# A table of steps for the pieces around a scan, and fp8 products in place of fp32 transposes

## The chip, the core and the metric

The kernel runs as one program on one NeuronCore of a Trainium2 chip. The core has a matrix engine (PE; its weight loads are shown apart as PEld), a vector engine (DVE), an activation engine (ACT), a general engine (POOL) and a queue that only issues transfers (SP). Each works through its own list of instructions in the order in which the program wrote them. The metric is device time in microseconds (us), start to end of one execution; the median of three runs is given for the kernel before.

## What is computed

The input x is 4 images of 64 x 64 tokens with 96 channels, fp32. Two layers follow.

Layer 0 is a group norm over the whole image (32 groups of 3 channels), a layer norm, a projection of 96 to 4896 columns, and a scan over the 4096 tokens with 16 states per channel:

```python
h_new = d * (A_t * h) + d * (B_t * u)          # 96 channels x 16 states
y     = g_t * jnp.sum(C_t * h_new, axis=-1)    # g = sigmoid(gate)
x     = x + (y @ W_out + b_out)
```

Layer 1 is attention without a softmax (so K and V can be contracted first, into one matrix per image), then a feed-forward network whose inputs, weights and hidden values are rounded to fp8 (5 exponent bits, 2 mantissa bits) and whose sums are rounded to fp16:

```python
t = t + attn(ln(t));   t = t + ffn(ln(t))      # ffn: q8(ln) @ q8(W1), relu, q8, @ q8(W2)
```

## The kernel before, in words

**Chunks, tiles and steps.** A batch image is cut into 8 chunks of 512 tokens, so there are 32 chunks. The 96 x 16 = 1536 states of a chunk are cut into 12 tiles of 128 partitions (3 groups of 32 channels times 4 groups of states). One *step* works on one tile, so a chunk is 12 steps and the main loop has K = 384 steps. Step numbers below are relative to the first step of the chunk that a piece belongs to; what counts for who meets whom is the number modulo 12, here called the *residue*.

**What a step holds.** For tile s the program writes, in this order: the B product of tile s+3 (PE, `b_proj`) and its copy out of PSUM (ACT, `b_copy`), the A product of tile s+1 (`a_proj`), the C product of tile s (`c_proj`), a copy of the last state (ACT, `keep`), the product B*u of tile s+2 (POOL, `b_mul`, L751), the scan of tile s (DVE, L767), A*d of tile s+1 (DVE, `a_mul`, L760), C*h of tile s (DVE, `c_mul`, L791), and then the pieces that were registered for this step. Each of the three products is three matmuls of 128 x 512 (high and low parts of fp32 numbers). For 4 of the 12 tiles, `ON_POOL`, C*h is done by ACT (`c_copy`, L797) and POOL (`c_mul_pool`, L800) instead of DVE, one step later. The A product has two PSUM banks: A of tile s+1 can start when the scan of tile s-1 has ended. B has one bank, which `b_copy` frees. All pieces share three banks named M, which go round.

**The pieces.** They are registered with `at(step, function)`, and run in the order of registration within a step.
- `front`: `load_x`, the group norm's `centre` and `scale` (POOL), layer norm (`stats` on DVE, `rstd` on POOL, `apply` on ACT), `transpose` (PE), `affine` and `upper` (ACT), `low` (DVE, then three transfers on SP), the products for d, u and gate with their outputs (`d_out` ACT, `du_out` DVE, `gate_out` ACT), and `write` and `read` (SP), which spread d and d*u over partitions through DRAM. They all run ahead of the chunk's first step.
- `gather` (a POOL transfer that adds) folds the four groups of states into one.
- `tail`: `state_sum` (PE), `gated` (DVE), the output product, `residual`, the norm of layer 1 with its `apply`, `transpose`, `keep` and `spill` (SP, to DRAM), and the Gram matrix of the chunk.
- `attn_matrix`, once per image, turns the Gram matrix into one 97 x 96 matrix.
- `ffn`, one image (96 steps) later: `fetch` (SP), `attention` (PE), `residual`, norm, `apply` (L371, ACT; L378, DVE, in the last image), `transpose` (L996, PE, fp32), `quant_in` (L1000, ACT, PSUM to fp8), three times `hidden` and `relu`, `project_out` (L1035), `round_out`, `bias_out` and `total` (POOL, L1049 and L1055) and `store`.
- `group_norm` for the next image: 8 times `sums`, then a chain of small pieces.

**Buffers.** x of a chunk lies in one of 15 buffers from `load_x` until `total` of its feed-forward part. The queue order on SP is the order in which the steps write its transfers.

**Start and end.** The first six steps are laid out by a small planner (`planned_start`) with costs and due times, and what is left after step 384 by another (`end`): it orders the remaining pieces by rank and by when they can start. `Plan.LOOK` is how far apart two start times still count as equal.

The order of instructions, and so everything below, is set by the program text alone; there is no scheduler behind it.

Of the kernel before, what the change touches and what calls it, by code (L numbers as in the profile page):

```python
# [21 lines left out]
J = 4  # L22
# [15 lines left out]
FRONT = -22  # L38
SUMS = -28
FFN0 = 28  # L40
ON_POOL = (1, 3, 6, 10)
# [4 lines left out]
def conv_attn_hybrid_kernel(  # L46
# [35 lines left out]
        "xn2": 1, "xq": 1, "h16": 1, "hr": 1, "hq": 1, "y16": 1, "yb": 1, "o": 1,  # L82
# [106 lines left out]
    xa_t, xal_t = [], []  # L189
    for r in range(2):  # L190
        t = const.tile([P, J, CA], F32, tag=f"xa{r}", name=f"xa{r}")
        nc.gpsimd.memset(t[:, :, C:CA], 1.0)
        xa_t.append(t)
        t = const.tile([CA, J, P], F32, tag=f"xal{r}", name=f"xal{r}")
        nc.gpsimd.memset(t[C:CA], 1.0)
        xal_t.append(t)

# [12 lines left out]
    w2_sb = sb("xn2", [C, HID], F32, "w2_sb")  # L210
# [125 lines left out]
    class LayerNorm:  # L336
# [32 lines left out]
        def apply(self, dst, src):  # L369
            for j in range(J):  # L370
                nc.scalar.activation(  # L371
                    dst[:, j, 0:C], src[:, j, :], AF.Identity,
                    bias=self.nmr[:, j : j + 1], scale=self.r[:, j : j + 1],
                )

        def apply_vector(self, dst, src):
            for j in range(J):
                nc.vector.tensor_scalar(  # L378
                    dst[:, j, 0:C], src[:, j, :], self.mv[:, j, 0:1], self.r[:, j : j + 1],
                    ALU.subtract, ALU.mult,  # L380
                )
# [182 lines left out]
    def group_norm(b, s0):  # L564
        q = {}

        def make():
            q["g"] = GroupNorm(b)
            q["g"].first()

        def call(name, *args):
            getattr(q["g"], name)(*args)

        when = [s0 + SUMS + NT * n for n in range(NCH)]
        if b == 1:
            when = [8, 15, 22, 29, 36, 43, 50, 57]
        if b > 1:
            at(when[0] - 7, load_gx, b, 0)  # L580
        at(when[0] - 2, make)
        for n in range(NCH):
            if n:
                at(max(when[n] - 7, when[n - 1]), load_gx, b, n)
            at(when[n], call, "sums", n)
        for n, name in ((1, "moments"), (2, "mean"), (4, "root"), (6, "diagonal"), (8, "spread"),
                        (8, "spread_out")):
            at(when[-1] + n, call, name)
# [107 lines left out]
    def front(b, i, s0, f=None):  # L696
        s = s0 + FRONT
        if f is None:
            f = Front(b, i)
            if (b, i) not in xt:  # L700
                at(s - 3, load_x, b, i)
            at(s, f.centre, nc.gpsimd)
            at(s + 1, f.scale, nc.gpsimd)
            at(s + 2, f.stats)
            at(s + 3, f.ln.rstd)
            at(s + 5, f.apply)
            at(s + 7, f.transpose)
            at(s + 8, f.affine)
            at(s + 9, f.upper)
            at(s + 9, f.low)  # L710
            at(s + 12, f.proj, 2)
            at(s + 13, f.d_out)
            at(s + 13, f.proj, 0)
            at(s + 14, f.du_out)
            at(s + 14, f.write)
            at(s + 15, f.read)
        at(s + 20, f.proj, 1)
        at(s + 21, f.gate_out)
# [89 lines left out]
    def state_sum(g, last=None, first=None):  # L808
# [17 lines left out]
        {"A": 2, "B": 1, "C": 1, "M": 3, "xal": 2, "xat": 1, "bu": 5, "h": 3, "rep": 2,  # L826
# [5 lines left out]
    def tail(b, i, s0):  # L832


        nm, g = f"{b}_{i}", b * NCH + i
        v, ln = {}, LayerNorm(1e-5, f"a_{nm}")
# [46 lines left out]
        def gram_add():  # L883
            nc.gpsimd.tensor_tensor(grams[b], grams[b], v["add"], ALU.add)

        plan = [
            (5, state_sum, g), (6, gated), (7, project_out), (8, residual), (8, ln.stats, t),
            (9, ln.rstd), (12, ln.apply, xa, t), (14, transpose), (15, keep), (16, spill),
            (21, gram), (22, gram_out),
        ]  # L890
        if i:
            plan.append((23, gram_add))
        for n, fn, *args in plan:
            if s0 + n < K:
                at(s0 + n, fn, *args)
        if s0 + plan[-1][0] < K:
            return
# [3 lines left out]
        job, a = end.job, None  # L901
        if s0 == K:
            for sh, late in ((0, 0.0), (2, 0.0), (3, 2.4)):
                w = job(f"wait{sh}", late, lambda: None)
                a = job("PE", 0.5, state_sum, g, sh, sh > 0, after=[a, w],
                        take=["B:y"] if sh == 0 else [])
            a = job("DVE", 0.7, gated, after=[a], free=["B:y"])
            a = job("PE", 0.5, project_out, after=[a], take=["B:o"])
            a = job("DVE", 0.56, residual, after=[a], free=["B:o"])
            a = job("DVE", 1.1, ln.stats, t, after=[a], take=[f"mv:a{i}"])  # L910
            a = job("POOL", 1.3, ln.rstd, False, after=[a])
        else:
            job("wait", 0.0, lambda: None, take=[f"mv:a{i}"])
        if s0 == K:
            applied = job("DVE", 1.3, ln.apply_vector, xa, t, after=[a], free=[f"mv:a{i}"])
        else:
            applied = job("ACT", 1.55, ln.apply, xa, t, free=[f"mv:a{i}"])
        a = job("PE", 0.4, gram, after=[applied, end.last.get("gram")], take=[f"B:g{i}"])
        end.last["gram"] = job("DVE", 0.25, gram_sum, after=[a], free=[f"B:g{i}"])
        a = job("PE", 0.45, transpose, after=[applied], take=[f"C:a{i}"])  # L920
        a = job("ACT", 0.57, keep, after=[a], free=[f"C:a{i}"], take=[f"xat:{i}"])
        end.last[b, i] = job("SP", 0.5, spill, after=[a], late=2.5, free=[f"xat:{i}"])
# [4 lines left out]
    def attn_matrix(b, s0):  # L927
# [31 lines left out]
        for n, (args, out) in enumerate(chain):  # L959
            if s0 < K:  # L960
                at(s0 + 24 + n, mm, *args)
                at(s0 + 24 + n, out)
# [4 lines left out]
    def ffn(b, i, s0):  # L967
# [21 lines left out]
        def apply():  # L989
            v["xn"] = tile_of("xn2", "bu", [P, J, C], F32, "xn2")  # L990
            (ln.apply_vector if b == B - 1 else ln.apply)(v["xn"], t)

        def transpose():
            ps = v["ps"] = bank("C" if phase["end"] else "M", [C, TC], f"xq_ps_{nm}")
            for j in range(J):
                nc.tensor.transpose(ps[:, j * P : (j + 1) * P], v["xn"][:, j, :], ident)  # L996

        def quant_in():
            v["xq"] = tile_of("xq", "h", [C, TC], F8, "xq")
            nc.scalar.activation(v["xq"], v["ps"], AF.Copy, saturate=False)  # L1000
# [7 lines left out]
        def relu(m):  # L1008
            if m == 0:
# [47 lines left out]
        def store():  # L1057
            nc.sync.dma_start(out_v[b, i], v["o"])

        plan = [  # L1060
            (min(-4, K - 4 - s0) if b < B - 1 else 0, fetch),
            (0, attention), (1, residual), (1, ln.stats, t), (2, ln.rstd),
            (5, apply), (7, transpose), (8, quant_in),
            (9, hidden, 0), (10, relu, 0), (11, hidden, 1), (12, relu, 1),
            (13, hidden, 2), (14, relu, 2), (15, project_out), (16, round_out),
            (17, bias_out), (18, total), (19, store),
        ]
        done = [fn for n, fn, *args in plan if s0 + n < K]
        for n, fn, *args in plan:
            if s0 + n < K:  # L1070
                at(s0 + n, fn, *args)
# [5 lines left out]
        assert relu not in done  # L1077
        if fetch in done and attention not in done:
            end.hold(f"xal:{nm}")

        def job(engine, cost, fn, *args, **kw):
            if fn not in done:
                return end.job(engine, cost, fn, *args, **kw)
            return None
# [8 lines left out]
        a = job("DVE" if vector else "ACT", 1.3 if vector else 1.55, apply, after=[a], take=[f"bu:x{nm}"], free=[f"mv:{nm}"])  # L1093
        a = job("PE", 0.45, transpose, after=[a], take=[f"C:{nm}"], free=[f"bu:x{nm}"])
        a = job("ACT", 0.6, quant_in, after=[a], take=[f"h:{nm}"], free=[f"C:{nm}"] if a else [])
        r, h, c = [], None, None
        for m in range(NK):
            h = job("PE", 0.24, hidden, m, after=[a, h], take=[f"M:{m}{nm}"], free=[f"h:{nm}"] if m == 2 else [])
            c = job("ACT", 0.57, round_hidden, m, after=[h, c], take=[f"rep:{nm}"] if m == 0 else [],
                    free=[f"M:{m}{nm}"])  # L1100
            r.append(job("DVE", 0.3, relu_vector, m, after=[c]))
        a = job("ACT", 1.5, quant, after=r, take=[f"bu:q{nm}"], free=[f"rep:{nm}"])
        a = job("PE", 0.5, project_out, after=[a], take=[f"A:y{nm}"], free=[f"bu:q{nm}"])
        a = job(*(("DVE", 0.56) if i % 2 else ("ACT", 0.48)), round_out, after=[a], take=[f"xs:{nm}"], free=[f"A:y{nm}"])
# [10 lines left out]
    def planned_start():  # L1115
        plan = Plan({"A": 2, "B": 1, "C": 1, "D": 1, "M": 3, "bu": 5, "h": 3})
        plan.LOOK = 0.8
# [32 lines left out]
        calm = land("calm", 29.0)  # L1150
# [77 lines left out]
        a = mm(0.5, second.transpose, after=[a, land("then", 38.0)], key="M:x2")  # L1228
# [36 lines left out]
    for b in range(B):  # L1265
        for i in range(NCH):
# [4 lines left out]
            for n, sh in ((7, 1), (10, 2), (13, 3)):  # L1271
                if g < N - 1 or sh == 1:
                    at(s0 + n, gather, g, sh)
            at(s0 + NT, tail, b, i, s0 + NT)
            s = s0 + NCH * NT + FFN0
            at(s - 4 if b == B - 1 else min(s, K) - 4, ffn, b, i, s)
        if b + 1 < B:
            group_norm(b + 1, b * NCH * NT)
        at((b + 1) * NCH * NT, attn_matrix, b, (b + 1) * NCH * NT)
# [82 lines left out]
```

## Time and profile before

| what | value |
|---|---|
| runs | 1212.67, 1214.04, 1214.79 us; median 1214.04 us |
| profiled execution | 1214.51 us, of which the span of instructions is 1212.8 us |
| mean granted PE clock | 0.989 |
| DVE busy | 1125.7 us (93%) |
| PE busy (ends modelled) | 1155.5 us (95%) |
| POOL busy | 1031.6 us (85%) |
| ACT busy | 809.9 us (67%) |
| first scan starts, last scan starts | 30.7 us, 1134.3 us |

A row of the timeline reads: start in us, duration in us, engine, source line, operation, output and inputs by the program's names, shapes, number of instructions merged into the row, and in brackets the idle time before it with what ended it. On DVE the durations overlap by some 0.08 us, so the distance from start to start is what an instruction costs. A row of the windows reads: the stretch and its length, then for PE, PEld, DVE, ACT and POOL busy us with the number of instructions, then the granted clock, the transfers' busy share and GB/s.

### The profile page before, as it was taken

The numbers are of one execution on the slowest core, as the hardware profiler recorded it, in microseconds if no ns is written. First come the engines' busy times: TensorE is split into PE (matmuls) and PEld (weight loads), VectorE is DVE, ScalarE is ACT, GpSimd is POOL, SyncE is SP. The second block draws the span as 40 slices with busy tenths as digits, with TensorE's granted clock in tenths as the row PEclk, the third lists the DMA queues.
The fourth block names the chain that finished last, engine by engine and source line by source line (L and its number), as shares of the span: only waits on it lengthen the run. The fifth ranks groups of instructions, "written<-read, shape, count | busy, mean of one in ns | idle before, by whom it ended". The sixth has DMA issues, their size and how long they took to land. (4 is left out here: it accounts for less than half of the span.)

```text
span 1212.8 us, 19189 instructions
## 1 busy us (share of the span) xinstructions
PE 1155.5 (95%) x5888; PEld 872.8 (72%) x5888; DVE 1125.7 (93%) x2103; ACT 809.9 (67%) x1812; POOL 1031.6 (85%) x1171
## 2 busy tenths in 40 slices
PE   6899999999999999999999999999999999999884
PEld 5677777777777777777777777677777777777652
DVE  6799999999999999999999999999999999999794
ACT  4655656655565787777777777777777777776574
POOL 3988878888888888999999888999999899988654
PEclk8999999999999999999999999999999999999998
DMA  7656767677776676677667766766776667666221
GB/s 185 141 133 145 165 151 164 147 161 164 168 160 151 153 166 151 154 168 176 159 151 164 172 154 146 174 154 149 154 174 154 154 158 174 153 145 142 66 66 40
DMA packets 104289, 182.14 MB, mean 150 GB/s; under 512 B 42637, under 2 KB 50769, under 8 KB 104186
## 3 DMA queue, kind: packets, MB, share of 16 engines
q1 hardware_dynamic: 90060, 106.96, 36.5%
q0 software_dynamic: 13536, 73.93, 30.2%
q8 instruction: 47, 0.77, 0.3%
q14 instruction: 56, 0.46, 0.1%
q10 hardware_dynamic: 590, 0.02, 0.0%
HBM read 69.12 MB, written 24.77 MB: 77 GB/s over the span
## 5 line engine op out<-in xcount | busy, mean ns | idle before, releaser
L751 POOL TENSOR_TENSOR bu<-bu,rep 128x512 f32<-128x512 f32 x384 | 557.7, 1496 | 14.7 <-ACT bu L748 9.2
L748 ACT ACTIVATE bu<-Bps,b_bac 128x512 f32<-128x512 f32 x384 | 263.7, 687 | 286.0 <-PE Bps L244 269.0
L767 DVE TENSOR_TENSOR_SCAN h<-Aps,state,bu 128x512 f32<-128x512 f32 x336 | 426.4, 1269 | 13.2 <-POOL bu L751 3.5
L760 DVE SCALAR_TENSOR_TENSOR Aps<-Aps,b_bac,rep 128x512 f32<-128x512 f32 x384 | 282.5, 736 | 25.1 <-PE Aps L244 24.6
L244 PE MATMUL Bps<-xs,w 128*128 128x512 f32 x768 | 268.1, 430 | 3.7 <-ACT bu L748 3.4
L244 PE MATMUL Aps<-xs,w 128*128 128x512 f32 x768 | 249.6, 406 | 14.2 <-DVE h L767 13.3
L800 POOL TENSOR_TENSOR ch<-ch,h 128x512 f32<-128x512 f32 x128 | 193.5, 1512 | 2.6 <-ACT ch L797 2.4
L244 PEld LDWEIGHTS Aps<-xs,w 128*128 128x128 f32 x768 | 138.6, 189 | 70.5 <-DVE h L767 42.3
L244 PEld LDWEIGHTS Bps<-xs,w 128*128 128x128 f32 x768 | 129.4, 191 | 46.5 <-issue 24.3
L244 PE MATMUL Aps<-xl,w 128*128 128x512 f32 x384 | 152.6, 397 | 0.3 <-DMA w<-w 0.3
L244 PE MATMUL Bps<-xl,w 128*128 128x512 f32 x384 | 151.8, 395 | 0.0
L244 PE MATMUL Dps<-xs,w 128*128 128x512 f32 x384 | 121.1, 397 | 0.0
L244 PE MATMUL Cps<-xs,w 128*128 128x512 f32 x384 | 120.8, 395 | 0.0
L806 POOL DMA_DIRECT2D ch<-ch x94 | 89.0, 947 | 15.1 <-DMA ch<-ch 11.5
L791 DVE SCALAR_TENSOR_TENSOR ch<-Dps,b_bac,h 128x512 f32<-128x512 f32 x128 | 94.7, 740 | 0.5 <-PE Dps L244 0.4
L791 DVE SCALAR_TENSOR_TENSOR ch<-Cps,b_bac,h 128x512 f32<-128x512 f32 x128 | 95.0, 742 | 0.0
L244 PEld LDWEIGHTS Aps<-xl,w 128*128 128x128 f32 x384 | 72.4, 188 | 18.4 <-DMA w<-w 1.0
L244 PEld LDWEIGHTS Bps<-xl,w 128*128 128x128 f32 x384 | 72.5, 189 | 17.5
L244 PEld LDWEIGHTS Dps<-xs,w 128*128 128x128 f32 x384 | 72.4, 189 | 17.5
L244 PEld LDWEIGHTS Cps<-xs,w 128*128 128x128 f32 x384 | 72.3, 188 | 17.5
L244 PE MATMUL Dps<-xl,w 128*128 128x512 f32 x192 | 76.0, 396 | 0.0
L244 PE MATMUL Cps<-xl,w 128*128 128x512 f32 x192 | 75.7, 394 | 0.0
(196 smaller groups left out, 2056.0 us busy)
## 6 DMA issues: line engine op xcount, KB each, us to landing
ch<-ch POOLq DMA_DIRECT2D x94, 768.0 KB, 6.5
rep<-ddd SPq DMA_DIRECT2D x124, 384.0 KB, 6.4
ddd<-dd SPq DMA_DIRECT2D x31, 384.0 KB, 3.0
xl<-lo SPq DMA_DIRECT2D x62, 128.0 KB, 2.4
x<-in_x_dram SPq DMA_DIRECT2D x32, 192.0 KB, 2.9
xatd<-xat SPq DMA_DIRECT2D x32, 192.0 KB, 3.1
xal<-xatd SPq DMA_DIRECT2D x32, 192.0 KB, 5.8
out_dram<-o SPq DMA_DIRECT2D x32, 192.0 KB, 2.1
```

The source lines that it names most:

```text
L244: nc.tensor.matmul(ps, lhsT=wt[:, n], rhs=mv, start=(n == 0), stop=(n == 2))
L748: nc.scalar.activation(self.bu, self.b_ps, AF.Identity, bias=self.bias(0))
L751: nc.gpsimd.tensor_tensor(self.bu, self.bu, rep[self.b, self.i][:, 1, self.cg], ALU.mult)
L760: nc.vector.scalar_tensor_tensor(self.a_ps, self.a_ps, self.bias(1), rep[self.b, self.i][:, 0, self.cg], ALU.add, ALU.mult,)
L767: nc.vector.tensor_tensor_scan(self.h, self.a_ps, self.bu, 0.0 if self.i == 0 else state[self.sh, self.cg], ALU.mult, ALU.add,)
L791: nc.vector.scalar_tensor_tensor(self.slot(), self.c_ps, self.bias(2), self.h, ALU.add, ALU.mult)
L800: nc.gpsimd.tensor_tensor(self.ch, self.ch, self.h, ALU.mult)
L806: nc.gpsimd.dma_start(chs[g, 0], chs.pop((g, sh)), accum_op=ALU.add)
```

## The change

One dictionary `AT` takes the place of the step numbers that were spread over `front`, `tail`, `ffn` and `group_norm`. In steps relative to the chunk's first step, before and after:

| piece | before | after | piece | before | after |
|---|---|---|---|---|---|
| load_x | -25 | -39 | rstd_a | 21 | 21 |
| centre, scale | -22, -21 | -25, -24 | apply_a | 24 | 22 |
| stats, rstd | -20, -19 | -22, -22 | transpose_a, keep, spill | 26, 27, 28 | 33, 34, 39 |
| apply | -17 | -21 | gram, gram_out, gram_add | 33, 34, 35 | 24, 24, 26 |
| transpose, affine | -15, -14 | -14, -13 | fetch | 24 | 21 |
| upper, low | -13, -13 | -13, -12 | attention, residual_f | 28, 29 | 26, 26 |
| proj_d, d_out | -10, -9 | -9, -9 | stats_f, rstd_f | 29, 30 | 26, 27 |
| proj_u, du_out | -9, -8 | -9, -9 | apply_f | 33 | 29 |
| write, read | -8, -7 | -9, -6 | transpose_f, quant_in | 35, 36 | 30, 31 |
| proj_gate, gate_out | -2, -1 | -3, -1 | hidden 0, 1, 2 | 37, 39, 41 | 37, 31, 38 |
| gather 1, 2, 3 | 7, 10, 13 | 7, 11, 14 | relu 0, 1, 2 | 38, 40, 42 | 37, 33, 38 |
| state_sum, gated | 17, 18 | 18, 18 | project_f, round_out | 43, 44 | 40, 40 |
| project_out, residual | 19, 20 | 19, 19 | bias_out, total, store | 45, 46, 47 | 40, 46, 51 |
| stats_a | 20 | 20 | group norm's first sums | -28 | -31 |

(The pieces of `ffn` are counted from the first step of the same chunk one image later.) The tiles whose C*h is on POOL are 0, 2, 7, 8 instead of 1, 3, 6, 10. A helper, `place`, puts a group of pieces into the loop only if all of it lies before step K; the rest goes to the end's planner, whose jobs leave out what is done. `attn_matrix` now starts at 15 steps after its image's end, not 24.

In `ffn`, the norm's `apply` writes fp8 straight into a 128-column tile whose last 32 columns are zero, and the four fp32 transposes become four fp8 products with an fp8 identity:

```diff
-FRONT = -22
-SUMS = -28
-FFN0 = 28
-ON_POOL = (1, 3, 6, 10)
+AT = { "load_x": -39, "centre": -25, ... "sums": -31, }
+ON_POOL = (0, 2, 7, 8)
...
+    ident8 = const.tile([P, P], F8, name="ident8")
+    nc.gpsimd.tensor_copy(ident8, ident, saturate=False)
...
+        t = const.tile([P, J, P], F8, tag=f"xn8{r}", name=f"xn8{r}")
+        nc.gpsimd.memset(t, 0.0)
+        xn8_t.append(t)
...
         def apply():
-            v["xn"] = tile_of("xn2", "bu", [P, J, C], F32, "xn2")
-            (ln.apply_vector if b == B - 1 else ln.apply)(v["xn"], t)
+            v["xn"] = xn8_t[i % 2]
+            (ln.apply_vector if b == B - 1 else ln.apply)(v["xn"], t, saturate=False)
 
         def transpose():
-            ps = v["ps"] = bank("C" if phase["end"] else "M", [C, TC], f"xq_ps_{nm}")
+            ps = v["ps"] = bank("C" if phase["end"] else "M", [P, TC], f"xq_ps_{nm}")
             for j in range(J):
-                nc.tensor.transpose(ps[:, j * P : (j + 1) * P], v["xn"][:, j, :], ident)
+                nc.tensor.matmul(
+                    ps[:, j * P : (j + 1) * P], lhsT=v["xn"][:, j, :], rhs=ident8,
+                    start=True, stop=True,
+                )
 
         def quant_in():
             v["xq"] = tile_of("xq", "h", [C, TC], F8, "xq")
-            nc.scalar.activation(v["xq"], v["ps"], AF.Copy, saturate=False)
+            nc.scalar.activation(v["xq"], v["ps"][0:C], AF.Copy, saturate=False)
...
+    def place(plan, s0):
+        done = set()
+        for group in plan:
+            if max(s0 + AT[name] for name, *_ in group) < K:
+                for name, fn, *args in group:
+                    at(s0 + AT[name], fn, *args)
+                    done.add(fn)
+        return done
...
     def planned_start():
         plan = Plan({"A": 2, "B": 1, "C": 1, "D": 1, "M": 3, "bu": 5, "h": 3})
-        plan.LOOK = 0.8
+        plan.LOOK = 0.6
```

In the end's planner the fp8 tile has a ring of its own with two buffers (before, `xn` took one of the five `bu` buffers there). Costs and due times of the planners are otherwise as before.

## The prediction

> **What bounds the kernel now.** I read the page's busy shares first, then the windows of single chunks, then DVE's timeline in one of them.
>
> ```profile
> PE 1155.5 (95%) x5888; PEld 872.8 (72%) x5888; DVE 1125.7 (93%) x2103; ACT 809.9 (67%) x1812; POOL 1031.6 (85%) x1171
> ```
>
> Two engines are near full, so the question is what a chunk waits for. Three windows, each one chunk long, from first scan to first scan: without layer 1, with it, and with it but without the group norm's sums.
>
> ```profile
> 241.03:273.82 32.79, 32.60 (x155) 24.51 (x154) 31.91 (x53) 19.15 (x49) 29.43 (x33) 1.00 0.75 167
> 549.29:583.91 34.62, 34.26 (x180) 26.29 (x179) 33.38 (x62) 25.51 (x51) 31.84 (x37) 1.00 0.74 164
> 898.38:932.91 34.53, 34.17 (x177) 26.05 (x176) 33.38 (x62) 25.32 (x58) 32.30 (x38) 1.00 0.73 162
> ```
>
> Pitch is 32.8 us for most of chunks 1 to 9 and 34.55 us from 10 to 29. DVE's timeline in the second window shows where its 1.2 us of idleness are:
>
> ```profile
> 553.10 0.73 DVE L760 SCALAR_TENSOR_TENSOR Aps<-Aps,b_bac,rep 128x512 f32<-128x512 f32 x1
> 553.93 1.28 DVE L767 TENSOR_TENSOR_SCAN h<-Aps,state,bu 128x512 f32<-128x512 f32 x1
> ...
> 558.46 1.28 DVE L767 TENSOR_TENSOR_SCAN h<-Aps,state,bu 128x512 f32<-128x512 f32 x1
> 560.60 0.76 DVE L760 SCALAR_TENSOR_TENSOR Aps<-Aps,b_bac,rep 128x512 f32<-128x512 f32 x1 [0.86 <-PE Aps L244]
> ...
> 568.70 0.73 DVE L760 SCALAR_TENSOR_TENSOR Aps<-Aps,b_bac,rep 128x512 f32<-128x512 f32 x1
> 569.35 0.68 DVE L840 TENSOR_TENSOR yg<-y_ps,gate 96x512 f32<-96x512 f32 x1
> 569.94 1.27 DVE L767 TENSOR_TENSOR_SCAN h<-Aps,state,bu 128x512 f32<-128x512 f32 x1
> ```
>
> First, in tile 1, whose C*h is on POOL, A*d of tile 2 is followed at once by the scan that reads it: 0.83 us from start to start. With another instruction between (568.70) A*d costs 0.65. So 0.18 to 0.2 us are lost at tiles 1, 3 and 10; at tile 6 `gated` fills the place. Second, in step 4 DVE waits 0.95 us for A (2.14 us from scan to A*d, against 1.19 elsewhere), 0.57 without layer 1. Nothing else is idle: DVE sets the pitch, and PE is just behind it. Summing PE's shortest start-to-start spacing of each kind of instruction over the second window gives 33.1 of 34.6 us, and 32.7 in the third.
>
> **The change, part by part.**
>
> *ON_POOL and DVE's order.* No DVE work is added or removed. DVE's pieces now stand in residues 0 (`low`), 2 (norm, `residual`, norm), 3, 6, 7 and 8, so tiles 0, 2, 7 and 8 all have a piece between A*d and the scan: 3 x 0.19 = 0.57 us less per chunk. `residual` and `stats_a` no longer touch (0.58 against 0.47 from start to start): 0.1 less. If the wait at step 4 went too, DVE's floor is 34.62 - 0.95 - 0.57 - 0.1 = 33.0 us with layer 1, and 32.79 - 0.57 - 0.57 - 0.1 = 31.5 without.
>
> *fp8 transposes.* The rows:
>
> ```profile
> L996 PE MATMUL xq_ps<-ident,xn 128*96 128x128 f32 x128 | 22.1, 283 | 4.3 <-DVE xn L378 4.3
> L1035 PE MATMUL y_ps<-w_q,hq 128*128 128x96 fp8e5 x384 | 23.0, 212 | 8.1 <-ACT hq L1029 6.6 <-ACT hq L1015 0.7 <-DVE mv_f L348 0.7
> L1035 PEld LDWEIGHTS <-hq 128*128 128x128 fp8e5 x384 | 18.7, 101 | 17.8 <-ACT hq L1029 9.9 <-issue 6.8 <-ACT hq L1015 0.8
> ```
>
> An fp32 transpose costs 0.109 us from start to start; an fp8 product of 96 columns with its own 128-column weights 0.043, so 0.057 for 128 columns: 4 x 0.052 = 0.2 us of PE per chunk. [...] The row decides: twelve such loads pass in 0.54 us. PE's floor becomes 33.1 - 0.2 = 32.9 us with sums, 32.5 without[...]. ACT's `apply` and `quant_in` move as many elements: nothing. At the start, `ident8` and two memsets (rows of 0.2 to 0.5 us) fall on POOL before it idles 7.16 us until 14.1 us: nothing.
>
> *The moves, against PE.* Both engines now have a floor of 33 us, but they must agree step by step: A of tile s+1 waits for the scan of s-1, so PE leads by 1.5 to 1.8 us at most. By residues, at 2.1 us of PE per step and the pieces' rows: steps 6 and 7 ask PE for 3.4 + 3.2 us (`transpose_f`, `state_sum`; `hidden1`, `project_out`) and DVE for 3.1 + 2.3, so a lead of 1.2 us is used up; step 2 gives back 1.1 (DVE 4.3, PE 3.2). `d_out`, `proj_u`, `du_out` share step 3, and `gated` shares a step with `state_sum`; the long steps 2 and 6 on DVE cover both.
>
> *Waits added on ACT.* Step 5 holds two sums (1.5 us) and `apply_f` (1.55) with copies of 0.9: 4.0 us against 2.5 of DVE. Queued behind is `b_copy`, which frees B's one bank, so PE can stand up to 0.9 us in step 7. In step 7 `hidden1` needs `quant_in` of the same step: up to 0.5 us. Between floor and floor + 1.4 I take +0.9 for chunks with sums (10 to 20): 33.9; for 21 to 29 +0.5: 33.5. Without layer 1: floor 31.5, taken 31.9.
>
> *Waits added on POOL.* `rstd` now stands in the step of its `stats`: POOL waits until 2.8 us into step 2, then works 1.8, `gather3` 0.7, `gram_add` 0.4, `b_mul`, `c_mul_pool`, `rstd_f` (1.3 + 1.3 + 1.8) and the next `b_mul` until 11.4 us; that scan comes at 12.4. Covered by 1 us; each us beyond costs one per chunk.
>
> *Waits added on SP.* `load_x` asks at step -39 for a buffer that `total` of 15 chunks earlier leaves at -38. Behind it on SP are `fetch`, `load_gx` and `low`'s three transfers. See the third rival. `read` stands later, but its data is ready only after `write` has landed; 6 steps remain for its 6.4 us. `spill` and `store` have nobody close behind.
>
> *Start and end.* LOOK and the POOL tiles reshuffle the first six steps: -2 to +2 us, taken 0. At the end one more `transpose_a`, `keep`, `spill` falls to the planner: +0.5. `xn` on DVE there:
>
> ```profile
> L378 DVE TENSOR_SCALAR xn<-x,mv_f,rstd_f 128x96 f32<-128x96 f32 x32 | 14.0, 501 | 0.0
> ```
>
> 24 of the 32 take 0.32 us, 8 take 0.92 to 1.06 beside a POOL instruction of 0.91. [...]
>
> *Sum.* Chunks 1 to 9: 9 x (31.9 - 32.8) = -8.1. Chunks 10 to 20: 11 x (33.9 - 34.6) = -7.7; 21 to 29: 9 x (33.5 - 34.55) = -9.5. Chunks above the plain pitch (3, 4, 10, 13, 18, 21: norm and attention chains of small tiles, 13.9 us in all) keep most: -3. Chunks 30, 31: -1. End +0.5, start 0. Together -28.8. The profiled execution took 1214.5 us (span 1212.8 and 1.7 around it), 0.5 over the median: 1185.7 from it, 1185.3 from 1214.04. I give 1186.
>
> **The rivals.**
> *A: both floors are met.* FFN chunks at 33.1, others at 31.6: 20 x -1.45 + 9 x -1.2 = -40, chains -6: 1168. For it: DVE was packed without a gap wherever it didn't wait. Against: PE has never run below 1.5 us of slack per chunk.
> *B: PE and ACT stand where DVE stood.* The waits of step 5 and 7 come in full: FFN chunks 34.3, others 32.3: 20 x -0.28 + 9 x -0.5 - 2 = -12: 1202. For it: M's three banks go round in a new order, which I could not cost.
> *C, slower: SP waits and attention is late.* Now `fetch` goes out 3.3 us after a chunk's first scan (621.77 against 618.47), lands 5.8 later, and attention starts 2.6 us after that (in the chunk before: issued at 587.29, attention at 595.73).
>
> ```profile
> 615.87 1.19 POOL L1055 TENSOR_TENSOR o<-x,yb 128x384 f32<-128x384 f32 x1
> ...
> 621.77 0.50 SPq L977 DMA_DIRECT2D xal<-xatd  x1
> ```
>
> After the change it stands behind `load_x`, which waits for `total`: this ends 1.4 us before the scan, so `fetch` goes at about -0.7, lands at 5.1, and attention, two steps earlier than before, wants it at 5.0. DVE asks for the result only at 7.7, so 1.3 us are covered. Each us more costs one in each of the 17 chunks 11 to 27. It decides at 1.3 + 28.8 / 17 = 3.0 us of a later `total`; at 3.5 us the time is 1186 + 37 = 1223. For it: POOL is 92% busy and has new waits. Against: `total` keeps residue 10, with `bias_out` 6 steps ahead.
> *D: no change,* if gains and waits cancel: 1214.
>
> **How the numbers follow.** Forecast 0.52 (its own range 1178 to 1195), A 0.16, B 0.20, C 0.09, D 0.03. 0.2% is about what a measurement of this kernel can tell from no change. Faster 0.88, same 0.03, slower 0.09. The range leaves out half of A below 1168 and all of C and D: 1168 to 1207.
>
> **What would show it.** Right: the 0.83 us from A*d to the scan gone from DVE, pitch near 31.9, 33.9 and 33.5; the wait of A*d on A at step 4 gone or moved to step 7; four fp8 products in 0.23 us; DVE's busy time as before. Wrong: attention or the scan's `bu` waited for each chunk (SP, POOL), or ACT's `b_copy` as the releaser of PE's B.

## The result, and the profile after

The changed kernel takes 1202.94 us (median; 1202.05 to 1206.4), the kernel before 1213.96 in the same series: a ratio of 0.9915, 95% interval 0.9894 to 0.9937. It is faster by 11 us, where 28 us had been forecast. The sign and the range (1168 to 1207) held; the size didn't. The profiled execution took 1203.4 us, its span 1201.3 is 11.5 less than before.

The page of the changed kernel, busy shares of the span:

```profile
PE 1150.0 (96%) x5888; PEld 875.1 (73%) x5888; DVE 1116.6 (93%) x2103; ACT 813.7 (68%) x1812; POOL 1034.8 (86%) x1174
```

The same windows of one chunk as for the kernel before (without layer 1; with it and the group norm's sums; with it and without the sums).

```profile
275.61:307.33 31.72, 31.66 (x152) 24.47 (x152) 31.48 (x54) 18.26 (x36) 28.54 (x31) 1.00 0.77 165
547.46:582.25 34.79, 34.40 (x179) 26.26 (x179) 33.04 (x62) 25.83 (x51) 31.93 (x37) 1.00 0.75 164
960.22:993.70 33.48, 33.48 (x175) 25.80 (x175) 32.95 (x62) 25.11 (x57) 31.92 (x37) 1.00 0.74 164
```

The first and third kind fell by 1.1 us, as forecast. The second didn't fall: 34.8 us, with DVE idle for 1.75 us of it. In the third PE has no idle time left (33.48 of 33.48 us; the ends of its products are modelled). The forecast's terms beside what the two traces show, from the start of a chunk's first scan to the next one's:

| term | forecast us | measured us |
|---|---|---|
| start: time of the first scan; chunk 0 | 0 | +0.3; +2.8 |
| chunks 1 to 9 | -8.1 | -3.3 |
| chunks 10 to 20 (with the sums) | -7.7 | -1.1 |
| chunks 21 to 29 (without) | -9.5 | -9.9 |
| chunks above the plain pitch | -3 | (within the rows above) |
| chunks 30, 31 | -1 | +0.4 |
| end | +0.5 | -0.9 |
| sum | -28.8 | -11.5 |

What DVE, ACT and PE do in a chunk with sums, steps 5 to 7, in the timeline of each (PE without the projections):

```profile
563.94 0.66 ACT L532 ACTIVATE gx_ps<-gx_ps,gmc 96x512 f32<-96x512 f32 x1 [1.21 <-PE gx_ps L503]
564.53 0.19 ACT L532 ACTIVATION_READ_ACCUMULATOR gx_ps<-gx_ps,gmc 96x1 f32 x1
564.75 0.57 ACT L532 ACTIVATE gx_ps<-gx_ps 96x512 f32<-96x512 f32 x1
565.25 0.19 ACT L532 ACTIVATION_READ_ACCUMULATOR gx_ps<-gx_ps 96x1 f32 x1
565.34 1.53 ACT L394 ACTIVATE xn<-x,nmr_f,rstd_f 128x96 fp8e5<-128x96 f32 x4
```

```profile
565.85 1.30 PE L1038 MATMUL xq_ps<-ident,xn 128*128 128x128 fp8e5 x4
567.08 1.06 PE L832 MATMUL y_ps<-ch,fold 128*32 128x512 f32 x6
```

```profile
566.59 0.74 DVE L808 SCALAR_TENSOR_TENSOR ch<-Cps,b_bac,h 128x512 f32<-128x512 f32 x1
568.22 0.69 DVE L869 TENSOR_TENSOR yg<-y_ps,gate 96x512 f32<-96x512 f32 x1 [0.90 <-PE y_ps L832]
...
571.57 0.56 DVE L879 TENSOR_TENSOR x<-o_ps,x 128x384 f32<-128x384 f32 x1 [0.81 <-PE o_ps L874]
```

Read backwards: `gated` on DVE waits 0.90 us for `state_sum` on PE; PE starts that at 567.08, because the four fp8 products in front of it take 1.30 us (0.40 where they don't wait, in e2 below); they are stretched because each waits for one of the four pieces of `apply_f`, which start 0.36 us apart; and `apply_f` starts only at 565.34, because the group norm's two sums stand ahead of it on ACT in the same step.

In chunk 0 there is a second new wait, on ACT and then on PE:

```profile
57.64 1.54 ACT L394 ACTIVATE z<-z,nmr_c,rstd_c 128x96 f32<-128x96 f32 x4 [6.22 <-POOL nmr_c L382]
59.09 0.67 ACT L765 ACTIVATE bu<-Bps,b_bac 128x512 f32<-128x512 f32 x1
```

```profile
59.81 1.22 PE L267 MATMUL Bps<-xs,w 128*128 128x512 f32 x2 [6.58 <-ACT bu L765]
```

Chunk 2's first `apply` is now at step 24 - 21 = 3, so it is issued before the loop begins at step 6, and in ACT's order stands ahead of the next `b_copy`. It waits 6.2 us for POOL, which has split weights (until 52.6 us) and then works through chunk 2's `centre`, `scale` and `rstd`; B has one bank, so PE stands too. From 55 to 66 us the granted clock is 0.53 on average, for 0.69 in the kernel before. Behind the wait, from 59.8 to 65.6 us, three products of 128 x 512 take up to 1.28 us from start to start, for 0.70 from 66 us on; in e3 below, where this wait is gone, PE is so slow only from 57.5 to about 61 us. So a slower PE is part of what chunk 0 loses against e3. It is not shown to be part of what it loses against the kernel before, where PE is as slow from 56.5 to about 62.5 us, behind a wait of 2.71 us for the scan.

### The profile page after: what moved, and what is told of

It is laid out like the page before. It is cut to its first block, busy times and chain, and to the rows that moved or that the text cites. A ratio compares the mean times of both kernels' runs of the same rounds, so it can differ in the third digit from the quotient of the medians.

```text
span 1201.3 us, 19166 instructions
## 1 busy us (share of the span) xinstructions
PE 1150.0 (96%) x5888; PEld 875.1 (73%) x5888; DVE 1116.6 (93%) x2103; ACT 813.7 (68%) x1812; POOL 1034.8 (86%) x1174
## 5 line engine op out<-in xcount | busy, mean ns | idle before, releaser
L768 POOL TENSOR_TENSOR bu<-bu,rep 128x512 f32<-128x512 f32 x384 | 512.5, 1343 | 51.3 <-ACT state L794 37.6
L267 PE MATMUL Aps<-xs,w 128*128 128x512 f32 x768 | 242.6, 397 | 1.6 <-DVE h L784 1.5
L817 POOL TENSOR_TENSOR ch<-ch,h 128x512 f32<-128x512 f32 x128 | 172.7, 1349 | 13.3 <-ACT ch L814 9.9
L267 PEld LDWEIGHTS Aps<-xs,w 128*128 128x128 f32 x768 | 144.0, 188 | 38.3 <-DVE h L784 4.0
L267 PEld LDWEIGHTS Bps<-xs,w 128*128 128x128 f32 x768 | 126.5, 191 | 59.1 <-ACT bu L765 24.3
L808 DVE SCALAR_TENSOR_TENSOR ch<-Dps,b_bac,h 128x512 f32<-128x512 f32 x160 | 118.5, 741 | 0.1
L814 ACT ACTIVATE ch<-Cps,b_bac 128x512 f32<-128x512 f32 x96 | 66.0, 687 | 22.9 <-PE Cps L267 22.9
```

The source lines that it names most:

```text
L267: nc.tensor.matmul(ps, lhsT=wt[:, n], rhs=mv, start=(n == 0), stop=(n == 2))
L768: nc.gpsimd.tensor_tensor(self.bu, self.bu, rep[self.b, self.i][:, 1, self.cg], ALU.mult)
L808: nc.vector.scalar_tensor_tensor(self.slot(), self.c_ps, self.bias(2), self.h, ALU.add, ALU.mult)
L814: nc.scalar.activation(self.ch, self.c_ps, AF.Identity, bias=self.bias(2))
L817: nc.gpsimd.tensor_tensor(self.ch, self.ch, self.h, ALU.mult)
```

## The experiments

Theory: the change does what it should in a plain chunk (one without layer 1), and gives back more than half of the forecast gain in orders on ACT: the sums ahead of `apply_f`, and chunk 2's `apply` ahead of `b_copy`. Rivals: PE at 96% has no room for the transposes of `gx`; M's three banks; or the table's gain comes from elsewhere than I thought. Pitches below are of chunks 7, 19 and 28 (without layer 1; with sums; without sums), from each run's trace:

| kernel | us, median | ratio to before (95%) | plain | sums | no sums | chunk 0 | chunk 5 |
|---|---|---|---|---|---|---|---|
| before | 1214 | 1 | 32.81 | 34.62 | 34.54 | 41.8 | 32.8 |
| changed | 1202.9 | 0.9894 to 0.9937 | 31.72 | 34.87 | 33.47 | 44.6 | 34.8 |
| e1 sums28 | 1197.8 | 0.9850 to 0.9886 | 32.02 | 34.24 | 33.49 | 43.3 | 34.3 |
| e2 sums behind | 1191.8 | 0.9800 to 0.9840 | 31.72 | 33.92 | 33.46 | 44.3 | 34.8 |
| e3 apply c2 | 1201.2 | 0.9880 to 0.9913 | 31.71 | 34.87 | 33.47 | 41.1 | 36.4 |
| e4 before, pool | 1193.9 | 0.9817 to 0.9854 | 31.60 | 34.28 | 33.60 | 41.5 | 32.5 |
| e5 the same, whole | 1195.1 | 0.9825 to 0.9860 | 31.61 | 34.24 | 33.58 | 41.5 | 32.5 |
| e6 old pool | 1239.2 | 1.0186 to 1.0219 | 33.38 | 35.70 | 34.29 | 43.7 | 39.6 |
| e7 fp32 | 1205.8 | 0.9920 to 0.9952 | 31.73 | 34.97 | 33.66 | 43.4 | 36.3 |
| e8 behind + c2 | 1192.9 | 0.9795 to 0.9835 | 31.71 | 33.92 | 33.48 | 41.0 | 36.3 |
| e9 sums32 + c2 | 1190.3 | 0.9781 to 0.9817 | 31.72 | 34.02 | 33.47 | 41.4 | 35.1 |
| e10 e8 + make | 1191.3 | 0.9792 to 0.9829 | 31.71 | 33.93 | 33.47 | 41.2 | 33.9 |
| e11 pool 0378 | 1220.0 | 1.0033 to 1.0062 | 32.95 | 35.11 | 33.71 | 44.4 | 36.9 |
| e12 pool 12710 | 1228.7 | 1.0097 to 1.0139 | 32.59 | 35.47 | 34.06 | 44.1 | 37.5 |

**e1: the sums three steps later.**

```diff
-    "sums": -31,
+    "sums": -28,
```

> The changed kernel with one entry of the table put back: the group norm's sums three steps later (-28 for -31, step 8 of a chunk for step 5), the gx load and the moments move with them. Theory (the sums stand before apply_f on ACT in step 5, and PE's fp8 products of step 6 and the state_sum behind them wait for it): chunks 10 to 20 lose the 1.39 us by which they are longer than the chunks without sums (34.87 against 33.48), step 6 goes from 4.08 to about 3.1 and step 7 from 3.30 to about 2.87; 10 x 1.39 + 0.7 = 14.6 us less if step 8 has room for the sums, 10.7 us if they cost there what the forecast gave them (33.9): 1189 to 1193 us. Rival (the 0.5 us of PE work of the transposes of gx, which PE at 96% has no room for): the chunks stay within 0.5 us of 34.87, 1198 to 1203 us.

Measured 1197.81 us, in between. The waits went as the theory has it: step 6 took 3.09 us for 4.07, step 7 2.88 for 3.30. But the sums are not free at step 8: steps 10 and 1 grew from 2.49 to 2.86 and 2.82 us, and so they did in the plain chunks 6 to 9, which hold sums there too (31.7 to 32.0). The rival, that the chunks stay at 34.9, fails; the theory's sum was too high by what the new place costs.

**e2: the same step, behind `apply_f`.** This moves no work to another step; only the order within the step is turned, in every step that holds sums (also those of image 1, counted from 0, in chunks 0 to 4, where chunks 1 to 4 together change by 0.2 us).

```diff
-            at(when[n], call, "sums", n)
+            at(when[n] - 1, at, when[n], call, "sums", n)
```

> The changed kernel with the sums left in step 5, but issued behind apply_f there and no longer ahead of it; PE's order in step 5 and 6 hardly moves. Theory (order on ACT): apply_f starts 1.4 us earlier, the fp8 products of step 6 don't wait, chunks 10 to 20 fall by 0.9 to 1.4 us each, 1188 to 1194 us. Rival 1 (PE's own work of the transposes of gx): no change, 1201 to 1204 us. Rival 2 (a bank of M, which gx now holds 1.5 us longer): no change or slower, 1203 to 1215 us.

Measured 1191.80 us, 11 us less than the changed kernel, and 33.92 us in the chunks with sums: 0.95 less in each. ACT, PE and DVE in the same steps of the same chunk as above:

```profile
557.13 1.53 ACT L394 ACTIVATE xn<-x,nmr_f,rstd_f 128x96 fp8e5<-128x96 f32 x4
558.57 0.64 ACT L532 ACTIVATE gx_ps<-gx_ps,gmc 96x512 f32<-96x512 f32 x1
```

```profile
560.30 0.40 PE L1038 MATMUL xq_ps<-ident,xn 128*128 128x128 fp8e5 x4
560.63 1.06 PE L832 MATMUL y_ps<-ch,fold 128*32 128x512 f32 x6
```

```profile
561.77 0.69 DVE L869 TENSOR_TENSOR yg<-y_ps,gate 96x512 f32<-96x512 f32 x1
...
565.12 0.56 DVE L879 TENSOR_TENSOR x<-o_ps,x 128x384 f32<-128x384 f32 x1 [0.82 <-PE o_ps L874]
```

The products take 0.40 us for 1.30, and the wait of `gated` is gone. Both rivals fail: PE does the same work in the same steps, and `gx` holds its bank of M longer than before, not shorter. The wait of `residual` on `project_out` stays (0.82): it is PE's own, in the step that holds `hidden1` and `project_out`, and over this chunk PE is now busy without a gap (33.84 of 33.84 us).

**e3: chunk 2's first `apply` back inside the loop.**

```diff
-            at(s0 + AT[name], fn, *args)
+            second = name == "apply" and (b, i) == (0, 2)
+            at(7 if second else s0 + AT[name], fn, *args)
```

> The changed kernel with the first layer norm's apply of chunk 2 alone put back to step 7, where the kernel before has it, from step 3, which is before the loop. Theory (in ACT's order it stands ahead of b_copy of tile 9 and waits 6.2 us for POOL there, and PE waits for b_copy): chunk 0 goes from 44.6 us to about 41.8, 1200 us. Rival (POOL, which splits the weights, is late for chunk 2 anyway and the wait only moves): chunks 0 to 2 together stay within 1 us of 111.5 us, 1202 to 1204 us.

Chunk 0 fell by 3.5 us in the profile and chunks 0 to 2 together to 108.0 us, so the rival fails. The size is less sure: four profiles with the changed order have chunk 0 at 43.3 to 44.6 us, four with this edit at 41.0 to 41.4, so the order costs 2 to 3.6 us. The median fell by only 1.75 (1201.19), and the profiled execution (1203.1 us) is no shorter than that of the changed kernel (1203.4): its chunk 5 is 1.6 us longer and its stretch behind the last scan 2.3.

In chunk 5 the group norm of image 2 (counted from 0) begins while that of image 1 ends. ACT has `apply`, `diagonal` and `gc` in one step ahead of `b_copy`, `apply` itself starts late because it waits for POOL, and PE is idle for 2.8 us in both kernels. ACT in the changed kernel, then in e10 below, where `gc` is out of the way:

```profile
220.25 1.54 ACT L394 ACTIVATE z<-z,nmr_c,rstd_c 128x96 f32<-128x96 f32 x4 [1.78 <-POOL nmr_c L382]
```

```profile
216.71 1.54 ACT L394 ACTIVATE z<-z,nmr_c,rstd_c 128x96 f32<-128x96 f32 x4 [1.74 <-POOL nmr_c L382]
```

By an estimate from the windows below the 1.6 us are PE's clock, which fell behind the wait in e3's profile and not in the changed kernel's: 0.84, 0.50 and 0.81 over three times 2 us lack 1.7 us. It is not shown to follow from the edit: e7, which has chunk 2's `apply` where the changed kernel has it, fell in the same way (36.3). The windows of this run, then of the changed kernel:

```profile
220.00:222.00 2.00, 2.00 (x8) 1.59 (x9) 0.75 (x2) 0.77 (x2) 1.94 (x3) 0.84 0.42 142
222.00:224.00 2.00, 2.00 (x8) 1.66 (x7) 1.48 (x3) 0.32 (x1) 0.97 (x1) 0.50 0.89 256
224.00:226.00 2.00, 2.00 (x10) 1.67 (x9) 0.93 (x1) 1.43 (x5) 0.00 (x0) 0.81 1.06 212
```

```profile
222.00:226.00 4.00, 2.22 (x10) 1.81 (x11) 2.32 (x3) 2.55 (x9) 3.93 (x4) 1.00 0.68 181
226.00:230.00 4.00, 4.00 (x23) 2.45 (x21) 3.58 (x5) 2.44 (x7) 1.69 (x2) 1.00 1.01 240
```

**e4 and e5: POOL's tiles alone.** The other way round: the kernel before, with only the choice of POOL's tiles changed. In e4 the last tile of all lies on POOL and its product, due one step behind the loop, is left out; e5 keeps that tile on DVE.

```diff
-ON_POOL = (1, 3, 6, 10)
+ON_POOL = (4, 6, 8, 11)
...
-            self.on_pool = self.r in ON_POOL
+            self.on_pool = self.r in ON_POOL and k < N * NT - 1
```

> The kernel before with other tiles given to POOL and nothing else: residues 4, 6, 8 and 11 for 1, 3, 6 and 10, so that each of them has a piece on DVE between a_mul and the next scan. Theory (three gaps of 0.19 us in a chunk, in which the scan waits for the a_mul just before it, are a part of the gain by themselves): 0.57 us less in each of 31 chunks, up to 17.7 us: 1196 to 1205 us. Rival (the gaps were slack of PE, which is busy for 95% of the span, or POOL's four products now meet its other work of steps 4 to 8 and b_mul is late): no change or slower, 1212 to 1235 us.

> The kernel before with POOL's tiles at residues 4, 6, 8 and 11 as in the run with that name, but complete: there the product of the very last tile (residue 11, due one step behind the loop's end) was left out, here that one tile stays on DVE. Theory (where a tile of POOL has a piece on DVE between a_mul and scan, the gaps go): within 2 us of that run, 1192 to 1197 us, so more than the whole change brings. Rival (the missing product spared the end more than its own 1.3 us): 1198 to 1214 us.

1193.94 and 1195.08 us: four numbers in a tuple bring 19 us, more than the whole change. The plain pitch is 31.6 and that without sums 33.6 us, what the changed kernel reaches with the whole table. DVE in steps 3 and 4 of a plain chunk of e5:

```profile
278.80 0.73 DVE L760 SCALAR_TENSOR_TENSOR Aps<-Aps,b_bac,rep 128x512 f32<-128x512 f32 x1
279.44 0.74 DVE L791 SCALAR_TENSOR_TENSOR ch<-Dps,b_bac,h 128x512 f32<-128x512 f32 x1
280.10 1.27 DVE L767 TENSOR_TENSOR_SCAN h<-Aps,state,bu 128x512 f32<-128x512 f32 x1
281.29 0.73 DVE L760 SCALAR_TENSOR_TENSOR Aps<-Aps,b_bac,rep 128x512 f32<-128x512 f32 x1
```

Two things went. Of the 1.2 us that a plain chunk became shorter, 0.57 are the three gaps, the mechanism that I had counted first. The other half is the wait of A*d for A in step 4 (0.54 us before), which went too, though no piece of PE had moved: the tuple also moves C*h from one step of DVE to another (step 4 went from 4.77 to 3.42 us). That is why both runs lie below the 1196 to 1205 us that e4's theory gave for the gaps alone. The table's other entries show no further gain in these chunks, and the changed kernel has new waits in chunk 0, in chunk 5 and at the sums. What its entries would bring with e5's four tiles was not run.

**e6: the changed table with POOL's old tiles.**

```diff
-ON_POOL = (0, 2, 7, 8)
+ON_POOL = (1, 3, 6, 10)
```

> The changed kernel with the POOL tiles of the kernel before (residues 1, 3, 6, 10 for 0, 2, 7, 8), all else as changed. In the new table residues 3 and 6 have a piece on DVE behind a_mul, 1 and 10 have none. Theory (gaps): two gaps of 0.19 us in each of 31 chunks come back, 11.8 us, 1210 to 1217 us, all of the change's gain. Rival (the table's other entries carry the gain, and which tiles POOL takes is no matter): 1200 to 1205 us.

1239.19 us: 36 us, three times the gaps. Both theories of mine were too small; the table and its tiles belong together.

**e7: fp32 transposes.** `apply_f` writes an fp32 tile (two buffers), and PE transposes that:

```diff
-                nc.tensor.matmul(
-                    ps[:, j * P : (j + 1) * P], lhsT=v["xn"][:, j, :], rhs=ident8,
-                    start=True, stop=True,
-                )
+                nc.tensor.transpose(ps[:, j * P : (j + 1) * P], v["xn"][:, j, :], ident)
```

> The changed kernel with layer 1's transposes as before (fp32, from an fp32 tile with two buffers) and all else as changed. Theory of the forecast (fp8 products spare PE about 0.2 us in a chunk of layer 1, and the chunks with the sums stand in PE's order): 21 chunks with 0.1 to 0.3 us more each, 1205 to 1209 us. Rival (the fp8 products wait for apply_f piece by piece, and DVE sets the other chunks): 1202 to 1204 us.

1205.79 us. The steady chunks say it more finely than the median: 33.66 for 33.47 without sums, 34.97 for 34.87 with them, so 9 x 0.19 + 11 x 0.10 = 2.8 us. (The medians differ by 2.85, within a spread of 4 us for each.) From the first of the four to the next product PE takes 0.53 us here and 0.33 with fp8 where nothing waits, so 0.20 us of PE's work are worth 0.19 us of a chunk, the 0.2 of the prediction, half of it hidden where they wait for `apply_f` anyway. It also shows that without sums the chunks are set by a path through PE, and no longer by DVE.

**e8: e2 and e3 together.**

> The changed kernel with both: the sums issued behind apply_f in step 5, and chunk 2's first apply back at step 7. Theory (two separate waits, of chunks 10 to 20 and of chunk 0): the two gains add, 11.1 and 1.8 us, 1189 to 1191 us; chunk 0 at about 41, chunk 5 about 1.6 us longer as in the run with the second alone. Rival (they share a wait): not below 1191.5 us.

1192.94 us (1189.4 to 1195.7). The chunks show both gains (41.0 in chunk 0, 33.92 with sums), and chunk 5 at 36.3; the median shows no gain over e2, as the rival had it. This one is not settled by the median: what e3's part saves is less than the spread, and some of that spread goes with PE's clock (see the end).

**e9 and e10: two ways to have it all.** e9 needs no change of order: one step earlier (with e3's lines). e10 is e8 with the `gc` of images 2 and 3 a step later.

```diff
-    "sums": -31,
+    "sums": -32,
```

```diff
-        at(when[0] - 2, make)
+        at(when[0] - (2 if b == 1 else 1), make)
```

> The changed kernel with the sums one step earlier (-32 for -31: step 4 of a chunk, in which ACT has only b_copy), and chunk 2's first apply at step 7. Theory (what costs is that the sums stand ahead of apply_f in one step; and in chunk 5 the second batch's first gc, with the diagonal and an apply in one step on ACT, keeps PE idle for 2.8 us, after which its clock was granted at 0.50 to 0.84 for some 5 us in three of the profiles): chunks 10 to 20 at 33.5 to 34.0 us, chunk 5 at 33 to 35 for 36.3, together 1186 to 1190 us. Rival (the sums' ACT time delays apply_f from there as well): chunks 10 to 20 at 34.5 to 35, 1196 to 1201 us.

> The changed kernel with the sums behind apply_f, chunk 2's first apply at step 7, and the second batch's gc one step later (64 for 63). Theory (in step 63 apply, diagonal and gc stand ahead of b_copy on ACT; without gc b_copy comes about 0.95 us earlier, PE idles less than 2 us and its clock is not lowered): chunk 5 at 33 to 34.5 us for 36.3, and 1186 to 1190 us with less spread than the run without it (1189.4 to 1195.7). Rival (another wait of chunk 5, for POOL's nmr_c, sets it): chunk 5 stays over 35.5 us, 1189 to 1196 us.

e9: 1190.32 us, chunks with sums at 34.02, at the edge of what was expected, so an earlier step does what the order within the step did. Its clock fell again in chunk 5 (0.79 and 0.78 in two windows of 4 us), behind a wait of 1.88 us. e10: 1191.26 us, a little above what was expected; chunk 5 is at 33.94, PE's wait there 1.94 us for 2.73, and its clock stayed at 1.00 in the one execution that was traced. Of the 2.4 us to e8, 0.8 are the order (e2, whose clock didn't fall either, has 34.75) and 1.6 the clock. The rest of the wait is the one that the rival names: `apply` waits 1.74 us for `nmr_c` of POOL.

e2, e8, e9 and e10 lie within 2.6 us and their intervals overlap: all beat the changed kernel by 10 to 13 us, and none is shown to be the best. They beat the kernel before by 21 to 24.

**e11: POOL's tile 3 for tile 2.** To tell the gaps from whatever made e6 so slow: here no gap comes back.

```diff
-ON_POOL = (0, 2, 7, 8)
+ON_POOL = (0, 3, 7, 8)
```

> The changed kernel with POOL's tile at residue 3 in place of 2. Both have pieces on DVE behind a_mul, so no gap of 0.19 us comes back, but step 2, the fullest of DVE (two or three pieces), then has a c_mul as well, and step 3 none. Theory of the gaps alone: within 2 us of the changed kernel, 1201 to 1206 us. Rival (what the choice of tiles does is to even out DVE's steps against PE's; A has two banks, so one long step can't be made up): step 2 goes from 2.76 to 3.4 (from 4.26 to 4.9 with layer 1) and step 3 doesn't give all of it back: 0.2 to 0.6 us in a chunk, 1208 to 1222 us.

1219.95 us, 17 us slower for one tile, and yet not for the reason given. Steps 2 and 3 cancel (3.42 for 2.76, then 2.47 for 3.13). The loss is in steps 5 to 7, and ACT shows why, in a plain chunk of this run and of the changed kernel:

```profile
293.46 1.54 ACT L394 ACTIVATE z<-z,nmr_c,rstd_c 128x96 f32<-128x96 f32 x4 [0.63 <-POOL nmr_c L382]
294.91 0.67 ACT L814 ACTIVATE ch<-Dps,b_bac 128x512 f32<-128x512 f32 x1
295.48 0.67 ACT L765 ACTIVATE bu<-Bps,b_bac 128x512 f32<-128x512 f32 x1
```

```profile
285.37 1.54 ACT L394 ACTIVATE z<-z,nmr_c,rstd_c 128x96 f32<-128x96 f32 x4
286.82 0.67 ACT L765 ACTIVATE bu<-Bps,b_bac 128x512 f32<-128x512 f32 x1
```

A tile on POOL also takes a `c_copy` on ACT (0.67 us), and at tile 3 this lands between `apply` and `b_copy`, 0.57 us from start to start; with DVE's c_mul now ahead of the statistics in step 2, `apply` starts 0.63 us late as well. The two add up: PE waits 1.31 us for B's bank in step 4 (0.06 in the changed kernel):

```profile
296.20 0.73 PE L267 MATMUL Bps<-xs,w 128*128 128x512 f32 x2 [1.31 <-ACT bu L765]
```

e6 has tile 3 on POOL too, and its plain steps 5 to 7 are the same: 2.94, 3.49, 3.01 us. In chunks of layer 1 e11 loses only 0.24 us, and there PE does not wait for B; what makes this part was not taken apart.

**e12: two gaps, without tile 3.**

```diff
-ON_POOL = (0, 2, 7, 8)
+ON_POOL = (1, 2, 7, 10)
```

> The changed kernel with POOL's tiles at residues 1, 2, 7 and 10: tiles without a piece on DVE behind a_mul at 1 and 10, and, other than in the two runs at 1220 and 1239 us, none at residue 3, where c_copy of POOL's tile would stand on ACT between the first apply and the next b_copy. Theory 1 (that c_copy is what made those two slow; a gap costs DVE 0.19 us): two gaps in each of 31 chunks, 11.8 us, 1210 to 1219 us, and steps 5 to 7 of a plain chunk stay at 2.49, 3.1 and 2.6. Theory 2 (DVE's steps have to be even: a step of 2.05 us is shorter than PE's 2.1 and can't be used): more than the gaps, 1220 to 1240 us, with waits on PE in the steps behind 1 and 10. Theory 3 (gaps cost nothing, since DVE has slack): 1200 to 1206 us.

1228.72 us, 26 more than the changed kernel. Steps 1 and 10 take 2.05 us, about 0.2 above what is left when the 0.65 us of c_mul go from 2.49. Step 5 is back at 2.49. But steady chunks are longer by 0.87, 0.60 and 0.59 us, of which the two gaps are 0.38. In a plain chunk the rest stands in steps 6 and 7 (3.19 and 2.96 us for 3.09 and 2.62), and the trace names a wait for it, on ACT and then on PE:

```profile
290.39 1.54 ACT L394 ACTIVATE z<-z,nmr_c,rstd_c 128x96 f32<-128x96 f32 x4 [0.53 <-POOL nmr_c L382]
```

```profile
292.56 0.73 PE L267 MATMUL Bps<-xs,w 128*128 128x512 f32 x2 [0.63 <-ACT bu L765]
```

It is e11's wait without the `c_copy`: on POOL the product of tile 1 now stands ahead of `rstd`, `apply` starts 0.53 us late, and `b_copy` behind it. Theory 1 fits in that step 5 is short again without `c_copy`, but `apply` has a second way to be late, and the price is more than twice what it gave. Theory 2 has the size, but no waits on PE behind steps 1 and 10. In chunks of layer 1 this wait is not there, and what their other 0.2 us are stays open. Chunks 2, 5, 9, 13 and 21 are longer by 1.1 to 2.7 us; these were not taken apart.

## Why the prediction was half right

**Right.** *ON_POOL and DVE's order*: the gaps went, the wait at step 4 went, and e5 reaches the same pitches by a choice of tiles alone. The durations of DVE's instructions add up to 1276.5 us in both kernels, as forecast; the profile shows 9 us less of busy time (1116.6 for 1125.7) because more of them overlap. *fp8 transposes*: 0.19 us (0.2) a chunk. The row was right: where nothing waits, each fp8 product takes 0.056 us from start to start, against 0.108 in fp32, and the load of its 128 columns of weights 0.098 us on average, against 0.128 for 96 columns in fp32. ACT's `apply` and `quant_in` take what they took: 0.456 us with fp8 output for 0.461 with fp32, and 0.594 for 0.593. *`xn` in fp8 on DVE*, for which nothing was counted: 8 of 32 took 0.91 to 0.98 us, each beside `yb` or `o` on POOL (0.91 to 1.00 us), and the other 24 0.30 to 0.36; in fp32, in the kernel before, it was 9, where I had counted 8, at 0.92 to 1.06. *Waits added on POOL and SP*: covered in the steady chunks; in the changed kernel DVE's waits for attention's product come to 2.9 us in all, so rival C fell. *End*: within 1.4 us, of a stretch that differs by 4 us from profile to profile, so this says little.

**Right in the number, not in the reason.** The pitch without sums is 33.47 us (33.5). The 0.5 over DVE's floor of 33.0 was to be `hidden1` waiting for `quant_in`; that is 0.1 us at most. What DVE waits for, 0.49 us in step 7, is `project_out`, a product of PE. PE's floor, put at 32.5 us without sums and 32.9 with them, was too low: PE has no idle time in 33.48 us without sums, nor in 33.84 with them (e2).

**Wrong: the step "Waits added on ACT".** It named the place, step 5 with the sums and `apply_f` in 4.0 us, but the wrong thing behind it. I wrote that `b_copy` waits and that PE stands in step 7; instead the fp8 products of step 6 wait for `apply_f`, `state_sum` stands behind them in PE's order, and `gated` behind that (0.90 us). I had followed the queue of ACT and left out the readers of `apply_f`. The term was +0.9 over a floor of 33.0 us, 33.9; measured 34.87. That e2 has 33.92 is luck: there no `b_copy` is late, and the 0.9 is DVE's wait for `project_out`.

**Wrong: "start 0".** An `apply` that moves ahead of the loop's first step moves ahead of every `b_copy` of the loop: PE waits 6.6 us, and chunk 0 is longer by 2 to 3.6 us (e3). I had listed the first six steps as a reshuffle and not asked what each moved instruction waits for there.

**Wrong: the chains' "-3", and chunk 5 in it.** The sum had the chains keep most of their excess, with 3 us gained. Chunk 5, which had none, is now 3.1 us over the plain pitch, from three pieces on ACT in one step and POOL's late `nmr_c`; e10 takes 0.8 of it back by the order. The excess of chunks 1 to 4 (6.5 us over 31.72, before 4.6 over 32.81), where image 1's sums stand at steps that the table doesn't move, was not taken apart.

**The account.** Of the 17 us between forecast and result, the rows of the table give 6.6 to chunks 10 to 20, 4.8 to chunks 1 to 9 (most of it in chunk 5), 3.2 to the start with chunk 0, 3 to the chains and 1.4 to chunks 30 and 31; the end and chunks 21 to 29 came out 1.8 better than forecast. The order on ACT costs more than its row shows: with it turned (e2), chunks 10 to 20 are 10.2 us shorter and lie 11.3 below the kernel before, for the 7.7 of the forecast and a part of the 3.

**Rival B** has the measured number, 1202, but not its mechanism: its chunks without layer 1 and without sums were to be at 32.3 and 34.3, and are at 31.7 and 33.5.

## What to carry to other kernels

When a piece is moved, follow both lines from it: what is queued behind it on its own engine, and who reads the result of each instruction that it now delays, on every other engine, up to the one that sets the pitch. A copy that frees a single bank (here `b_copy`) is the victim to look for first; chunk 0, chunk 5, e11 and e12 are four cases of it. And before a table of 54 entries is credited with a gain, put a small part of the change into the old kernel: here four tile numbers gave more than all of it.

## What was not expected of the hardware

*PE's clock after a short idle.* In chunk 5 PE waits once, for 1.9 to 3.7 us, in the eleven traces of the changed table; in the kernel before its longest wait there is 0.37 us. In some the clock then fell: e3's three windows above lack 0.16, 0.50 and 0.19 of 2 us each, 1.7 us in all. It fell so behind 2.7 to 2.8 us in e3, e7 and e8 (to 0.50, 0.65 and 0.50 in the lowest window of 2 or 4 us) and behind 1.9 in e9 (0.78), and stayed at 1.00 behind 2.8 and 2.7 us in the changed kernel and e2 and 1.94 in e10; in e1 three products took 0.70 us from start to start both before and behind a wait of 2.4. Behind the longest waits, 3.1 to 3.7 us in e6, e11 and e12, it fell each time (0.50, 0.71 and 0.68). Chunk 5 is 1.6 us longer in e8 (36.32) than in e2 (34.75), with the same order there. So the length of the wait does not settle it by itself: 1.88 us went with a fall in e9, and 2.81 us with none in the changed kernel. What else it depends on was not shown.

*The end.* The 76 to 80 us behind the last scan hold a clock of 0.81 to 0.91, and differ between kernels that issue the same there (76.0 at 0.91 in e8, 79.6 at 0.83 in e10). This is larger than what e8 and e10 were to gain over e2, and may be why their medians don't show it; one execution of each was traced. In e8 the five times go with the mean granted clock, from 1189.4 us at 0.987 to 1195.7 at 0.981: an estimate from these two, 0.006 of 1190 us, is 7 us, near the 6.3 between them.
